# Two chained attention layers on one core: the squares of the next image's transpose sent a step sooner, and turned in place

## The chip, the cores and the metric

The kernel runs on one core of a Trainium2 chip. The metric is the device time of one execution in microseconds. All data are 32-bit floats.

## The reference

Eight images of 32 x 32 pixels with 256 channels pass through two attention layers. N = 1024 pixels of an image are the tokens.

```python
# layer 0, four heads, for each image
xf = x.reshape(B, N, C)
q, k, v = split(einsum('bnc,cd->bnd', xf, W_qkv).reshape(B, N, h, 3 * C), 3)
atten = softmax(einsum('bihd,bjhd->bijh', q, k) * C ** -0.5, axis=2)
res = einsum('bijh,bjhd->bihd', atten, v).reshape(B, N, h * C)
x = einsum('bnd,dc->bnc', res, W_out) + b_out + xf
# layer 1, one head with 32 channels for f and g
f, g, v = x @ Wf + bf, x @ Wg + bg, x @ Wh + bh
y = gamma * softmax(g @ f^T) @ v + x
```

## The kernel before

**Folded weights and seven products.** For each head of layer 0 the query and key weights are multiplied once into one 256 x 256 matrix (`wqk`), and the value and output weights into another (`wvo`). `fold_weights(h)` returns five tasks: turn q, turn k, turn v (L291: `pwq`, `pwk`, `pwv`), and two multiplications (L307: `pwqk`, `pwvo`). The larger products are made as 2 x 2 blocks with seven block products and sums of blocks in place of eight products. The helper `seven` (L222) holds this: its matmuls are all on line 235 and its additions on VectorE all on line 252, so they are told apart by tile names. In `psx`, `psy` and `psz` (scores), `psx_q` and so on (queries) and `psx_y` and so on (attention times values) the letter is the PSUM bank; `e`, `u` and `v` are the intermediate sums in SBUF, and the result goes to `p`, `q` or `y`. Sums of operands come from VectorE: `xs` (L385, from x^T), `qs` (L492), `s`, `s2`, `s3`, `ss` (L560, from the exponentials), and `xt` (L401, from the rows of x, by `value_sums`). The profile shows `s2` and `s3` as `s` too.

**Steps.** The list `steps` holds pairs of a unit and a block of 512 query tokens. A unit is a head of layer 0 of an image, or the layer-1 attention of the image before. That one stands behind head 1 of the next image (for the seventh image, behind head 3 of the eighth). Layer 1 of the last image comes after the loop. In one step the scores of that unit and block are made, with the products of the step before and the projections (`po`, L617) of the step before that.

**Order.** On TensorE, VectorE and ScalarE the order of instructions is the program's own. For each step the loop collects tasks with a place, a number on a scale where the six score tasks stand at 0, 2, 4, 6, 8 and 10, sorts them by place and calls them:

```python
        for _, _, t in sorted(places, key=lambda x: x[:2]):
            t()
```

A VectorE instruction that waits thus holds all VectorE work behind it. DMAs are all issued from SyncE (SP in the profile) in one queue; where they stand in it, and which buffer of a pool a tile gets, a scheduler decides. A DMA waits on SP for its source, for the release of the tile that its destination takes, and for one of eight completion semaphores to come free.

**x^T.** Layer 0 needs x and its transpose `x0T` (tag `xT`, two buffers, shared with `x1T`, the transpose of layer 0's output). Image 0's is made on TensorE (`transpose_rows`). For the others `turn_rows` moves squares of 32 x 32 elements by DMA to the place that they have in the transpose, and VectorE then turns each square with a 32 x 32 transpose. The squares land in a scratch tile, the still unused query tile of the next image's head 0 (`q`, two buffers). The moves (L358) are 16 DMAs per image; the four transposes (L364) read `q` and write `x0T`. All this belongs to step (head 3, block 0), and is followed there by the four `key_sums` (L385). The same function also turns layer 0's output for layer 1, with the tile `fg` as scratch.

**Row sums.** `Layer0.sums` reduces the sums of a block of exponentials over the partitions on GpSimd (L573), sends a row of it to memory (`line`, L577) and reads it back as columns (`st`, L580). `invert` (L586) takes the reciprocals, which `project` multiplies in (L628).

Of the kernel before, what the change touches and what calls it, by code (L numbers as in the profile page):

```python
# [16 lines left out]
P = 128  # L17
# [3 lines left out]
def kernel(  # L21
# [51 lines left out]
    nc = tc.nc  # L73
    B, H, W, C = x.shape
    N = H * W
    HEADS = w_qkv.shape[1] // (3 * C)
    CK = w_f.shape[1]
    CC = C // P
    NT = N // P
    NB = 512  # L80
# [28 lines left out]
    def tile_of(tag, shape, name):  # L109
        return pools[tag].tile(shape, F32, tag=tag, name=name)  # L110


    rows, rows1 = {}, {}

    def load_x(b, parts=1):
        t = tile_of("rows", [P, NT, C], f"x_{b}")
        n = HT // parts
        for k in range(NBLK):
            for i in range(parts):
                nc.sync.dma_start(  # L120
                    t[:, k * HT + i * n : k * HT + (i + 1) * n, :].rearrange("p t c -> p (t c)"),
                    x_v[b][:, k, ts(i, n * C)],
                )
        rows[b] = t
# [156 lines left out]
    def fold_weights(h):  # L281

        wT, hold = [], []
        folded[h] = []

        def turn(i, what):
            w, _ = weights[h]
            pt = tile_of("psm", [P, NB], f"pw{what}_{h}")
            for d in range(CC):
                for c in range(CC):  # L290
                    nc.tensor.transpose(  # L291
                        pt[:, d * C + c * P : d * C + (c + 1) * P],
                        w[:, c, i * C + d * P : i * C + (d + 1) * P],
                        ident,
                    )
            if i != 1:
                hold.append(tile_of("y", [P, N], f"w{what}T_{h}"))
            t = hold[-1][:, ts(i % 2, NB)]
            copy_on(i, t, pt)
            wT.append(t.rearrange("p (d c) -> p d c", d=CC))  # L300

        def multiply(i, what):
            wqT, wkT, wvT = wT
            pm = tile_of("psm", [P, NB], f"p{what}_{h}")
            for c in range(CC):
                for d in range(CC):
                    nc.tensor.matmul(  # L307
                        pm[:, ts(c, C)],
                        lhsT=(wqT, wvT)[i][:, d, ts(c, P)],
                        rhs=wkT[:, d, :] if i == 0 else weights[h][1][:, d, :],  # L310
                        start=(d == 0),
                        stop=(d == CC - 1),
                    )
            t = const.tile([P, CC, C], F32, tag=f"{what}{h}", name=f"{what}{h}")
            copy_on(i, t.rearrange("p c e -> p (c e)"), pm)
            folded[h].append(t)
            if i == 0:
                t4 = const.tile([P, 4, P], F32, tag=f"wt{h}", name=f"wt{h}")
                sums = [t4[:, k, :] for k in range(4)]
                blocks = [t[:, c, ts(e, P)] for c in range(CC) for e in range(CC)]  # L320
                run(sum_b(sums, *blocks))
                wblocks[h] = b_operands(blocks, sums)

        tasks = [partial(turn, i, what) for i, what in enumerate(("q", "k", "v"))]
        tasks += [partial(multiply, i, what) for i, what in enumerate(("wqk", "wvo"))]
        return tasks
# [16 lines left out]

        return [partial(task, k, c) for k in range(NBLK) for c in range(CC)]

    def turn_rows(b, src, dst, layer, scratch):

        Q = 32  # L350

        def move(a):
            to, rows_v = (
                t.rearrange("p u n -> p (u n)").rearrange("p (s q) -> p s q", q=P)
                for t in (scratch(), src[b])
            )
            for q in range(P // Q):
                nc.sync.dma_start(to[ts(q, Q), :, ts(a, Q)], rows_v[ts(a, Q), :, ts(q, Q)])  # L358

        def piece(k, c):  # L360
            if b not in dst:
                dst[b] = tile_of("xT", [P, CC, N], f"x{layer}T_{b}")
            squares = scratch()[:, k, :].rearrange("p (t c q) -> p t c q", c=CC, q=P)
            nc.vector.transpose(  # L364
                dst[b][:, c, ts(k, NB)].rearrange("p (t q) -> p t q", q=P), squares[:, :, c, :]
            )

        return (
            [partial(move, a) for a in range(P // Q)],
            [partial(piece, k, c) for k in range(NBLK) for c in range(CC)],  # L370
        )

# [409 lines left out]
    def run(*lists):  # L782
        for l in lists:
            for t in l:
                t()
# [42 lines left out]
    turn_q, turn_k, turn_v, *multiply = fold_weights(0)  # L828
    sums = key_sums(0)
    run(transpose_rows(0, rows, xT_of, 0), [turn_q, turn_k, sums[0], turn_v], sums[1:3])  # L830
    run(multiply, sums[3:], queries, qsums)

    def is_l0(s):
        return s is not None and isinstance(s[0], Layer0)
# [1 line left out]
    def step(k):  # L836
        return steps[k] if 0 <= k < len(steps) else None
# [4 lines left out]
    for i, (a, blk) in enumerate(steps):  # L842
        l0 = isinstance(a, Layer0)
        one, two, nxt = step(i - 1), step(i - 2), step(i + 1)
        places = []

        def put(tasks, *at):
            assert len(tasks) == len(at)
            places.extend(zip(at, range(len(places), len(places) + len(at)), tasks))

        if l0:
            put(a.scores(blk), 0, 2, 4, 6, 8, 10)
        else:
            tasks, pieces = a.scores(blk)
            put(tasks, *((0.5, 2.4) if blk == 0 else (0.5, 2)))
            put(pieces, *((1.6, 3.9, 6.2, 6.5, 7.4, 8.4, 8.6) if blk == 0 else
                          (0.9, 2.7, 4.2, 5, 6.2, 6.8, 7.5)))
        if is_l0(two):
            u, k = two
            put(u.products_of[k][2:], 1 if l0 else 0)  # L860
            put([partial(u.invert, k)], 2.9 if l0 or blk == 1 else 1.9)
            put(u.project(k), *((3, 7) if l0 else (2, 6) if blk == 0 else (3, 7)))
        if is_l0(one):
            u, k = one
            sums, keys = u.sums(k)
            u.products_of[k] = u.products(k)
            put(sums[:2] + sums[3:], *((2.2, 3.2, 4.2) if l0 else (0.8, 2.2, 4.5)))
            put(sums[2:3], 5.2 if l0 else 5.5)
            put(keys, *((6.2, 8.2) if l0 else (7.6, 9.6)))
            put(u.products_of[k][:2], *((5, 9) if l0 else (4, 7)))  # L870
        elif one is not None:
            put(one[0].products(one[1]), *((3, 5, 7, 9) if l0 else (1, 4, 6, 8)))
        if i == 0:
            fold = fold_weights(1) + fold_weights(2) + fold_weights(3)
            put(fold, -2, -1, *[0.9 + 0.6 * n for n in range(len(fold) - 2)])
        if i == 1:
            put([partial(nc.vector.tensor_scalar, bh_sb, bh_sb, gamma_sb, None, ALU.mult)], 8.5)

        if is_l0(nxt) and blk == NBLK - 1:
            queries, qsums = nxt[0].queries()  # L880
            put(queries, *((2.5, 4.5, 6.5) if not l0 else
                            (1.5, 2.5, 4.5) if is_l0(two) else (0.5, 2.5, 5.5)))
            put(qsums, *((6.7, 6.9, 7.3, 7.6) if not l0 else
                          (5.4, 6.4, 7.2, 7.4) if is_l0(two) else (6.4, 7.2, 7.3, 7.4)))

        if l0 and a.h == 0 and blk == 0:
            put(residual(a.b), 5.3, 6.3, 7.3, 7.4)
        if l0 and a.h == 0 and blk == 1:
            put(value_sums(a.b), 1.4, 2.4, 3.4, 4.4)
        if l0 and a.h == 2 and blk == 0 and a.b + 1 < B:  # L890
            load_x(a.b + 1)
        if l0 and a.h == HEADS - 1 and blk == 0 and a.b + 1 < B:
            moves, pieces = turn_rows(a.b + 1, rows, xT_of, 0, step(i + 2)[0].q_tile)
            put(moves, 0.1, 0.2, 0.3, 0.4)
            put(pieces, 3.4, 4.4, 5.4, 5.6)
            put(key_sums(a.b + 1), 6.4, 6.6, 7.2, 7.4)

        if l0 and a.b > 0 and a.h == behind(a.b) - 1:
            if blk == 0:
                moves, pieces = turn_rows(a.b - 1, rows1, x1T_of, 1, step(i + 2)[0].fg_tile)  # L900
                put(moves, 0.1, 0.2, 0.3, 0.4)
                put(pieces, 5.4, 6.4, 7.2, 7.4)
            else:
                put(nxt[0].queries(), 1.4, 1.5, 3.5)
        if not l0 and blk == 0:
            put(a.values(), 0.9, 1, 3, 5, 8)
        if nxt is None:
            put(transpose_rows(B - 1, rows1, x1T_of, 1), 8.1, 8.2, 8.3, 8.4)
            put(final.queries(), 9, 9.1, 9.3)
        for _, _, t in sorted(places, key=lambda x: x[:2]):  # L910
            t()
# [136 lines left out]
```

## Time and profile before

| what | value |
|---|---|
| time of three runs, median (lowest to highest) | 2374.21 us (2373.25 to 2375.3) |
| span of the profiled execution | 2373.4 us |
| VectorE busy | 1616.1 us (68%) |
| ScalarE busy | 589.8 us (25%) |
| GpSimd busy | 236.4 us (10%) |
| matmul instructions | 10384 |
| matmul 128 x 128 by 128 x 256 | 0.379 us |
| VectorE tensor_tensor, 128 x 512 | 0.68 to 0.69 us |
| VectorE tensor_tensor, 128 x 1024 | 1.22 us |
| VectorE transpose, 128 x 512 | 0.70 us (28 for `x0T`) |
| issue of one 64 KB move on SP | 0.63 us, 112 for `q`, 112 for `fg` |
| landing of such a move after its issue | 2.3 us (median) |

Busy time is the sum over an engine's instructions. "Idle before" an instruction is the time that its engine stood still just ahead of it, and the name behind the arrow is what ended that time. Where a row has one releaser, the instruction named there finished last. The end of a matmul is modelled, so a TensorE row's duration of several matmuls reaches beyond the start of the next group; the spacing of starts is what counts. The granted TensorE clock was full for the whole span.

### The profile page before, as it was taken

To read this page: it belongs to the slowest core of one execution; us is meant where nothing else is said; L and a number is where in the kernel's file an instruction comes from. 1 tells how busy PE (TensorE), PEld (TensorE's weight loads), DVE (VectorE), ACT (ScalarE), POOL (GpSimd) and SP (SyncE) were. 2 spreads that over 40 slices of the span, in tenths; PEclk is the share of its full clock that TensorE was granted. 3 is DMA by queue.
4 is the path that set the end of the run, shared out by engine and by line. 5 is a ranking of instruction groups with operands and counts; after the bars stand their busy time and mean duration, and the time that the engine had idled before them with its cause. 6 is when DMAs were issued, how large, how long until landed. Compare 5 with 4: busy or idle time off the path is not lost.

```text
span 2373.4 us, 25982 instructions
## 1 busy us (share of the span) xinstructions
PE 2342.1 (99%) x10384; PEld 1923.1 (81%) x10384; DVE 1616.1 (68%) x2533; ACT 589.8 (25%) x945; POOL 236.4 (10%) x93
## 2 busy tenths in 40 slices
PE   8999999999999999999999999999999999999999
PEld 6888888778878788787887878878788787888877
DVE  5667777577775667757777567675776757766665
ACT  2222223222232122322223222232122322222232
POOL 0111110011110111101111011110011101001110
PEclk9999999999999999999999999999999999999999
DMA  3001010010100101001010010100101001000100
GB/s 118 1 1 18 1 36 1 18 18 10 27 1 18 19 19 19 1 18 19 19 18 1 19 18 19 18 1 18 19 19 19 1 22 15 1 1 1 19 10 29
DMA packets 161809, 38.34 MB, mean 16 GB/s; under 512 B 154320, under 2 KB 156368, under 8 KB 161680
## 3 DMA queue, kind: packets, MB, share of 16 engines
q1 hardware_dynamic: 161680, 36.59, 7.5%
q8 instruction: 84, 1.38, 0.2%
q14 instruction: 45, 0.37, 0.0%
HBM read 13.37 MB, written 8.52 MB: 9 GB/s over the span
## 4 chain that ended last, share of the span: by engine, by line
PE 86%; DVE 8%; SPq 3%; issue 1%; DMA 1%; POOL 1%; ACT 0%; DVEq 0%; POOLq 0%; ACTq 0%
PE psy L235 12%; PE psy_y L235 12%; PE pa_l L767 9%; PE po L617 8%; PE psx L235 8%; PE psz L235 8%; PE psx_y L235 8%; PE psz_y L235 8%; PE psy_q L235 3%; SPq L358 3%; PE psx_q L235 2%; PE psz_q L235 2%; PE pr_v_l L446 2%; PE pm_fg L426 1%; PE ps_l L688 1%; DVE m L565 1%
## 5 line engine op out<-in xcount | busy, mean ns | idle before, releaser
L573 POOL PARTITION_ALL_REDUCE rb<-rs x64 | 206.9, 3233 | 1908.3 <-DVE rs L571 1908.3
L521 ACT ACTIVATE p<-p 128x1024 f32<-128x1024 f32 x128 | 135.3, 1057 | 573.3 <-DVE p L252 573.3
L235 PE MATMUL psy<-qs,xs 128*128 128x256 f32 x1024 | 264.2, 380 | 12.1 <-DVE u L252 6.2
L235 PE MATMUL psx<-q,x0T 128*128 128x256 f32 x1024 | 262.8, 379 | 0.0
L235 PE MATMUL psz<-q,xs 128*128 128x256 f32 x1024 | 262.8, 379 | 0.0
L235 PE MATMUL psy_y<-s,xt 128*128 128x256 f32 x1024 | 242.4, 380 | 1.4 <-DVE xt L401 1.2
L617 PE MATMUL po<-wvo,y 128*128 128x256 f32 x1024 | 242.0, 379 | 0.0
L235 PE MATMUL psx_y<-p,x 128*128 128x256 f32 x1024 | 241.9, 379 | 0.0
L767 PE MATMUL pa_l<-v_l,s_l 128*128 128x257 f32 x1024 | 231.7, 381 | 2.3 <-DVE y L252 1.9
L235 PEld LDWEIGHTS psx<-q,x0T 128*128 128x128 f32 x1024 | 194.4, 190 | 43.0 <-issue 18.7
L235 PEld LDWEIGHTS psy<-qs,xs 128*128 128x128 f32 x1024 | 193.4, 190 | 43.4 <-DVE u L252 9.0
L617 PEld LDWEIGHTS po<-wvo,y 128*128 128x128 f32 x1024 | 194.5, 190 | 40.0 <-issue 15.1
L767 PEld LDWEIGHTS pa_l<-v_l,s_l 128*128 128x128 f32 x1024 | 193.7, 190 | 39.0 <-issue 12.7
L235 PEld LDWEIGHTS psx_y<-p,x 128*128 128x128 f32 x1024 | 194.6, 190 | 34.1 <-issue 8.6
L235 PEld LDWEIGHTS psy_y<-s,xt 128*128 128x128 f32 x1024 | 192.1, 190 | 31.9 <-issue 4.0
L235 PEld LDWEIGHTS psz<-q,xs 128*128 128x128 f32 x1024 | 194.6, 190 | 26.4
L252 DVE TENSOR_TENSOR u<-psy,e 128x512 f32<-128x512 f32 x128 | 88.3, 690 | 143.7 <-ACT e L258 75.0
L264 ACT ACTIVATE p<-psx 128x512 f32<-128x512 f32 x128 | 76.4, 597 | 409.4 <-PE psx L235 409.3
L252 DVE TENSOR_TENSOR v<-psy,e 128x512 f32<-128x512 f32 x128 | 87.9, 687 | 104.4 <-PE psy L235 104.2
L235 PE MATMUL psy<-qs,x0T 128*128 128x256 f32 x512 | 132.1, 380 | 3.2 <-DVE v L252 3.2
L628 DVE SCALAR_TENSOR_TENSOR x<-po,inverse,x 128x256 f32<-128x256 f32 x256 | 112.0, 479 | 17.3 <-PE po L617 7.7
L235 PE MATMUL psz_y<-ss,x 128*128 128x256 f32 x512 | 120.9, 379 | 0.0
(110 smaller groups left out, 3048.0 us busy)
## 6 DMA issues: line engine op xcount, KB each, us to landing
out_dram<-x SPq DMA_DIRECT2D x15, 512.0 KB, 2.6
x<-in_x_dram SPq DMA_DIRECT2D x14, 512.0 KB, 4.6
q<-x SPq DMA_DIRECT2D x112, 64.0 KB, 2.3
fg<-x SPq DMA_DIRECT2D x112, 64.0 KB, 2.3
w<-in_L_conv_W_qkv_dram SPq DMA_DIRECT2D x4, 768.0 KB
x<-in_x_dram SPq DMA_DIRECT2D x4, 256.0 KB, 4.1
w<-in_L_conv_W_out_dram SPq DMA_DIRECT2D x4, 256.0 KB, 8.6
line<-rb SPq DMA_DIRECT2D x64, 2.0 KB
```

Of the source, the lines that this page charges most:

```text
L235: nc.tensor.matmul(banks[k][:, ts(i, w)], lhsT=lhsT, rhs=rhs, start=first and n == 0, stop=True, skip_group_check=True,)
L252: nc.vector.tensor_tensor(dst, shaped(banks[k]), shaped(other), ALU.add)
L264: copy(outs["11"](), shaped(banks["x"]))
L358: nc.sync.dma_start(to[ts(q, Q), :, ts(a, Q)], rows_v[ts(a, Q), :, ts(q, Q)])
L426: nc.tensor.matmul(pm[:m], lhsT=w()[:, c, d * P : d * P + m], rhs=src()[:, c, ts(k, NB)], start=(c == 0), stop=(c == CC - 1),)
L446: nc.tensor.matmul(pm[:, ts(j, C)], lhsT=src()[:, c, ts(2 * t2 + j, P)], rhs=w()[:, c, :], start=(c == 0), stop=(c == CC - 1),)
L521: exp(both, both)
L565: tt(m, t[:, :, 0:2, :], t[:, :, 2:4, :], ALU.add)
L573: nc.gpsimd.partition_all_reduce(t, r.rearrange("p e i -> p (e i)"), P, bass_isa.ReduceOp.add)
L617: nc.tensor.matmul(pm[:, ts(j, C)], lhsT=self.y[blk][:, c, ts(2 * t2 + j, P)], rhs=folded[self.h][1][:, c, :], start=(c == 0), stop=(c == ...
L628: nc.vector.scalar_tensor_tensor(acc, pm[:, ts(j, C)], inverse[:, n : n + 1], acc, ALU.mult, ALU.add)
L767: nc.tensor.matmul(pm[:, : C + 1], lhsT=p[:, j, ts(ti, P)], rhs=v[:, j, : C + 1], start=(j == 0), stop=(j == NT - 1),)
```

## The change

Three things change.

1. For the next image's `x0T` (not for layer 1's `x1T`), `turn_rows` is called without scratch. Its moves go into the `x0T` tile itself, split by channel half: 32 DMAs of 32 KB for 16 of 64 KB. They belong to step (head 2, block 1) and not to (head 3, block 0). The four transposes read and write the same 128 x 512 piece of `x0T`. In step (head 3, block 0) they stand at places 0.4, 1.4, 2.4 and 4.4 (before: 3.4, 4.4, 5.4, 5.6), and the first key sum at 5.4 (before: 6.4), the second at 6.4 (before: 6.6).
2. The four sums `xt` of image 0 are made two in step 0 and two in step 1; before, all four in step 1. Those of other images are not moved.
3. The first two tasks of head 1's folding come between the second and the third task of head 0's queries, ahead of the loop; the third stands at -1 in step 0, and the others follow at the same distances as before.

```diff
-    def turn_rows(b, src, dst, layer, scratch):
+    def turn_rows(b, src, dst, layer, scratch=None):
...
-        def move(a):
-            to, rows_v = (
-                t.rearrange("p u n -> p (u n)").rearrange("p (s q) -> p s q", q=P)
-                for t in (scratch(), src[b])
-            )
+        def end():
+            if b not in dst:
+                dst[b] = tile_of("xT", [P, CC, N], f"x{layer}T_{b}")
+            return dst[b]
+
+        def flat(t):
+            return t.rearrange("p u n -> p (u n)").rearrange("p (s q) -> p s q", q=P)
+
+        def move(a, c=None):
+            to, rows_v = flat(end() if scratch is None else scratch()), flat(src[b])
+            if c is not None:
+                to, rows_v = to[:, ts(c, NT), :], rows_v[:, c::CC, :]
             for q in range(P // Q):
                 nc.sync.dma_start(to[ts(q, Q), :, ts(a, Q)], rows_v[ts(a, Q), :, ts(q, Q)])
 
         def piece(k, c):
-            if b not in dst:
-                dst[b] = tile_of("xT", [P, CC, N], f"x{layer}T_{b}")
-            squares = scratch()[:, k, :].rearrange("p (t c q) -> p t c q", c=CC, q=P)
-            nc.vector.transpose(
-                dst[b][:, c, ts(k, NB)].rearrange("p (t q) -> p t q", q=P), squares[:, :, c, :]
-            )
+            to = end()[:, c, ts(k, NB)]
+            if scratch is None:
+                nc.vector.transpose(to, to)
+            else:
+                squares = scratch()[:, k, :].rearrange("p (t c q) -> p t c q", c=CC, q=P)
+                nc.vector.transpose(to.rearrange("p (t q) -> p t q", q=P), squares[:, :, c, :])
...
-    run(multiply, sums[3:], queries, qsums)
+    fold = fold_weights(1) + fold_weights(2) + fold_weights(3)
+    run(multiply, sums[3:], queries[:2], fold[:2], queries[2:], qsums)
+    first_sums = value_sums(0)
...
         if i == 0:
-            fold = fold_weights(1) + fold_weights(2) + fold_weights(3)
-            put(fold, -2, -1, *[0.9 + 0.6 * n for n in range(len(fold) - 2)])
+            put(fold[2:], -1, *[0.9 + 0.6 * n for n in range(len(fold) - 3)])
+            put(first_sums[:2], 8.4, 9.4)
         if i == 1:
+            put(first_sums[2:], 1.4, 3.4)
...
-        if l0 and a.h == 0 and blk == 1:
+        if l0 and a.h == 0 and blk == 1 and a.b > 0:
             put(value_sums(a.b), 1.4, 2.4, 3.4, 4.4)
...
+        if l0 and a.h == 2 and blk == 1 and a.b + 1 < B:
+            moves, squares = turn_rows(a.b + 1, rows, xT_of, 0)
+            put(moves, *range(1, 9))
         if l0 and a.h == HEADS - 1 and blk == 0 and a.b + 1 < B:
-            moves, pieces = turn_rows(a.b + 1, rows, xT_of, 0, step(i + 2)[0].q_tile)
-            put(moves, 0.1, 0.2, 0.3, 0.4)
-            put(pieces, 3.4, 4.4, 5.4, 5.6)
-            put(key_sums(a.b + 1), 6.4, 6.6, 7.2, 7.4)
+            put(squares, 0.4, 1.4, 2.4, 4.4)
+            put(key_sums(a.b + 1), 5.4, 6.4, 7.2, 7.4)
```

More of the change, by code (lines that the diff above doesn't have):

```diff
@@ L360, in piece @@
         def piece(k, c):
-            if b not in dst:
-                dst[b] = tile_of("xT", [P, CC, N], f"x{layer}T_{b}")
-            squares = scratch()[:, k, :].rearrange("p (t c q) -> p t c q", c=CC, q=P)
-            nc.vector.transpose(
-                dst[b][:, c, ts(k, NB)].rearrange("p (t q) -> p t q", q=P), squares[:, :, c, :]
-            )
+            to = end()[:, c, ts(k, NB)]
[4 more added lines that the diff above has]
+                nc.vector.transpose(to.rearrange("p (t q) -> p t q", q=P), squares[:, :, c, :])
         return (
-            [partial(move, a) for a in range(P // Q)],
+            [partial(move, a, c) for a in range(P // Q)
+             for c in ((None,) if scratch else range(CC))],
             [partial(piece, k, c) for k in range(NBLK) for c in range(CC)],
@@ L891 @@
             load_x(a.b + 1)
+        if l0 and a.h == 2 and blk == 1 and a.b + 1 < B:
+            moves, squares = turn_rows(a.b + 1, rows, xT_of, 0)
+            put(moves, *range(1, 9))
         if l0 and a.h == HEADS - 1 and blk == 0 and a.b + 1 < B:
-            moves, pieces = turn_rows(a.b + 1, rows, xT_of, 0, step(i + 2)[0].q_tile)
-            put(moves, 0.1, 0.2, 0.3, 0.4)
-            put(pieces, 3.4, 4.4, 5.4, 5.6)
-            put(key_sums(a.b + 1), 6.4, 6.6, 7.2, 7.4)
+            put(squares, 0.4, 1.4, 2.4, 4.4)
+            put(key_sums(a.b + 1), 5.4, 6.4, 7.2, 7.4)
         if l0 and a.b > 0 and a.h == behind(a.b) - 1:
             if blk == 0:
-                moves, pieces = turn_rows(a.b - 1, rows1, x1T_of, 1, step(i + 2)[0].fg_tile)
+                moves, turned = turn_rows(a.b - 1, rows1, x1T_of, 1, step(i + 2)[0].fg_tile)
                 put(moves, 0.1, 0.2, 0.3, 0.4)
-                put(pieces, 5.4, 6.4, 7.2, 7.4)
+                put(turned, 5.4, 6.4, 7.2, 7.4)
             else:
```

## The prediction

> **What bounds the kernel now.** I read the busy table first, then TensorE's waits, then the timeline around one of those waits.
>
> ```profile
> PE 2342.1 (99%) x10384; PEld 1923.1 (81%) x10384; DVE 1616.1 (68%) x2533; ACT 589.8 (25%) x945; POOL 236.4 (10%) x93
> ```
>
> TensorE is busy for 2342.1 of 2373.4 us. The change neither adds nor removes a matmul, so only the 31.3 us of idle can move. The view of who waited for whom says where most of it lies (total, times, longest):
>
> ```profile
> PE psy L235 <- DVE u L252: 6.2, 7, 1.0
> PE psy L235 <- DVE p L252: 4.6, 6, 1.8
> PE psy L235 <- DVE v L252: 3.2, 7, 0.5
> PE psy L235 <- DVE qs L492: 1.3, 1, 1.3
> PE psy_y L235 <- DVE xt L401: 1.2, 1, 1.2
> ...
> DVE x0T L364 <- DMA q<-x: 27.1, 7, 5.1
> ```
>
> There are eight images, so seven hand-overs to a next image, and the first three rows and the last come six or seven times each. Filtered to windows, they all fall in step (head 3, block 0), where the next image's x^T is turned. The timeline of the second hand-over shows the mechanism (start, duration, engine, line; in brackets the idle before):
>
> ```profile
> 498.01 9.35 SPq L358 DMA_DIRECT2D q<-x  x14
> ...
> 504.30 1.22 DVE L560 TENSOR_TENSOR s<-ss,p 128x1024 f32<-128x1024 f32 x1
> ...
> 505.63 1.60 PEld L235 LDWEIGHTS psy_y<-s,xt 128*128 128x128 f32 x8
> 505.74 1.89 PE L235 MATMUL psy_y<-s,xt 128*128 128x256 f32 x8
> ...
> 509.14 0.71 DVE L364 STREAM_TRANSPOSE x0T<-q 128x512 f32<-128x512 f32 x1 [3.63 <-DMA q<-x]
> ...
> 509.78 0.65 DVE L252 TENSOR_TENSOR p<-psy,e 128x512 f32<-128x512 f32 x1
> ...
> 510.49 1.13 PE L235 MATMUL psy<-qs,xs 128*128 128x256 f32 x4 [0.27 <-DVE p L252]
> ...
> 516.07 1.13 PE L235 MATMUL psy<-qs,xs 128*128 128x256 f32 x4 [0.99 <-DVE u L252]
> ...
> 521.11 1.13 PE L235 MATMUL psy<-qs,x0T 128*128 128x256 f32 x4 [0.46 <-DVE v L252]
> ```
>
> The sixteen square DMAs go out one after another up to 507.36 and the last lands at 509.02. VectorE reaches the first transpose at 505.5, stands 3.63 us, and everything behind it is late: the read of a PSUM bank (p), then u, then v. Each holds TensorE once.
>
> **What the Trainium skill says.** "Perfetto Trace Analysis", section "Tensor Engine Instruction (MATMUL, LD_WEIGHTS)", says ACT and DVE are strict FIFO; the trace agrees, since p had its inputs by 504.2 (its psz group ran at 503.15) and ran at 509.78 behind the transpose. The same page, "DMA Instruction — HWDGE (DVE, Sync)", says that the profiled DMA instruction ends when the sequencer is free and does not contain the data movement: here 0.63 us of issue beside 2.3 us to landing. "DMA: Bandwidth & Descriptors", section "Rules for kernel authors", advises issuing early and waiting late; that is this edit. "VectorE: DVE Perf Modes", section "The three transpose paths", limits a VectorE transpose to 32x32 blocks; the rows show 0.70 us for 128x512.
>
> **The change part by part.**
>
> *Squares sooner (images 1 to 7).* 16 moves of 64 KB into the q tile become 32 of 32 KB into the x^T tile, and nothing on VectorE waits for them any more. In the built program image 1's moves stand right behind the load of x_1 (issued at 20.18 us), over 100 us ahead of their transposes. For images 2 to 7 the first waits for the last pr_v matmul of the layer-1 unit, which reads the old contents of that x^T slot: for image 2 the group at 408.49, done by 410.4. At the 0.67 us spacing of the larger moves 32 take 21.4 us, and they are done near 436, 60 us before the transposes. Removed per hand-over: 2.4 to 5.1 us of VectorE standing. On TensorE that is 6.2 + 4.6 + 3.2 = 14.0 us. A restart costs more than the idle shows: the four matmuls at 516.07 take 0.97 to the next group, where others take 0.86, so 20 restarts x 0.11 = 2.2. Together **16.2 us**, the most that this part can return.
>
> *Transposes earlier.* In VectorE's order the four transposes move from behind s, ss and s to: after u; after the second y; ahead of the reciprocal; behind the second ss. Walking the second hand-over with the row's durations (independent instructions start 0.09 us before the former ends): T0 at 496.4 and T1 at 499.4 fall in idle of 0.85 and 1.3 us. T2 does not: ss starts at 502.10, T2 at 503.23, so the reciprocal, the two x and s move by 0.62, and s ends at 506.14 instead of 505.52. The weights of psy_y<-s were loaded at 505.63, that is, as soon as s was there, so this is a **new wait**: TensorE starts at about 506.20 instead of 505.74, 0.46 and a restart of 0.11 to 0.2, say 0.6. The first hand-over has the same spacing (s at 214.28, psy_y at 215.72). 7 x 0.6 = **4.3 us lost**. Going on: p at 506.1 and 506.6, ss 507.2, T3 508.4, u_y 509.5 (behind ACT's exp), s 509.8, xs 511.0; u waits for its own matmuls and runs at 511.8 (TensorE needs it at 515.0), v at 516.4 (needed at 519.3). So none of p, u and v holds TensorE: net 16.2 - 4.3 = **11.9 us**.
>
> *In-place form.* No row shows it. Nearest is the same instruction from q, 0.70 us; bounds are the 0.61 spacing of dense tensor_tensor rows and twice the row, 1.4. I take 0.70; twice makes the new wait 1.3 us, 5 us more in all.
>
> *SP's queue.* 16 more issues x 7 x 0.67 = at most 75 us (a half-size issue costs between st's 0.36 and 0.63); SP waits 1483.8 us for the row sums alone. But order matters. In Layer1's block 0 seven moves stand ahead of the line DMA of head 1, block 1, and three between line and st:
>
> ```profile
> 418.12 0.23 SPq L577 DMA_DIRECT2D line<-rb  x1
> 419.31 0.36 SPq L580 DMA_DIRECT2D st<-line  x1
> 426.34 0.17 DVE L586 RECIPROCAL inverse<-st 128x4 f32<-128x4 f32 x1
> ```
>
> The seven end at 410.4 + 4.7 = 415.1, before the sums at 418.1: nothing lost. Three cost 2.0, so st goes out at 420.4 and lands (2.1 us) at 422.5, 3.8 ahead of its reader. The 22 left end at 435.5, before the output DMA's condition at 441.43. Cost: nothing, hidden by that slack. POOL's order is unchanged.
>
> *Image 0.* Two of the four xt sums move to idle VectorE time in step 0 (1.12 us idle ahead of 51.40), so the 1.2 us wait of psy_y for xt goes, with its restart **1.3 gained**. The folding of head 1 starts two tasks earlier: pwq and pwk fill the 0.78 us in which psy_q waited for v_q, but q and qs depend on v_q, not on these, so psy still starts at 26.18 and the idle there grows from 1.29 to 1.9. Pwv has moved ahead of it (0.43 us gained), but further on pwq, pwk and pwv now follow directly on a score group, and pwv waits for the copy of pwq behind v and p on VectorE, about 1.3 us where before 0.35 stood. Net **0.6 lost**, bounds 1.5 gained and 2.5 lost.
>
> Sum: -11.9 - 1.3 + 0.6 = **-12.6 us**; on the profiled span 2373.4 that is 2360.8, and on the median of the runs, 2374.2, it is **2361.6 us**.
>
> **The rivals.**
> 1. *New wait twice as large, or dear in-place transposes.* For: s is needed as soon as it is made. Gain 12.6 - 5 = 7.6: 2366.6 us.
> 2. *Hidden anyway.* The stretch holds the same VectorE work, and if u and v are late by its density rather than by the 3.63 us, only the p waits go (4.6 + 0.7), about eaten by the new 4.3: with image 0 the time is 2373 us. Against: the walk leaves VectorE 2 to 3 us ahead at u and v.
> 3. *Slower: st lands late.* Image 2 to 7's moves share SP and the DMA engines with st. If moves drained one at a time (2.3 us each), the ten ahead of it would hold st's data until 410.4 + 23 + 2.1 = 435.5, and L586 would stand 9.2 us with x, r_l and s_l behind it and TensorE waiting for PSUM. It decides from a delay of 4 us on, and turns the sum above 6 us. About 8 us on TensorE x 6 - 12.6 = +35: 2410 us. Against: 14 moves sent 0.67 apart landed 2.29 us after the last issue, so they overlap.
> 4. *The moves stay late.* If the x^T slot were freed later than the built order says, the transposes would wait as before: 2373 us.
>
> **How the numbers follow.** Forecast 0.72, rival 1 0.14, rivals 2 and 4 together 0.08, rival 3 0.06. The forecast's own spread is image 0's bounds (about -2 to +2) and the new wait (3 to 5 us, or nothing if s slips in): 2357 to 2365. With rival 1 and an edge for unknown sizes the range is 2356 to 2369 us. A difference of 0.2% (4.7 us) is about what can be told from none here: faster 0.87, same 0.07, slower 0.06.
>
> **What would show it.** The row "x0T <- DMA" goes from VectorE's waits; p, u and v go from TensorE's; a row psy_y <- s appears with 7 entries of about 0.5 us; psy_y <- xt is gone; L586 waits for no DMA; TensorE busy stays 2342. I am wrong if u and v keep holding TensorE, if L586 waits, or if the idle that went from the hand-overs turns up in image 0's first 50 us.

## The result, and the profile after

The changed kernel takes 2358.94 us (median of six runs, 2357.61 to 2360.93) beside 2374.9 us for the kernel before on the same chips (six runs, 2373.25 to 2376.75). The ratio is 0.9933, with a 95% interval of 0.992 to 0.9946. That is 16.0 us less; 12.6 us had been predicted. The profiled span fell by 16.5 us, from 2373.4 to 2356.9.

The busy line of the changed kernel's page:

```profile
PE 2336.5 (99%) x10384; PEld 1923.2 (82%) x10384; DVE 1617.1 (69%) x2533; ACT 590.7 (25%) x945; POOL 236.6 (10%) x93
```

VectorE does the same work as before, to 1 us. TensorE's busy time is 5.6 us lower with the same 10384 matmuls, which the prediction had excluded; the reason is further down. TensorE's waits in the changed kernel (total, times, longest; the row of the load of x at the start, and rows of 0.4 us and less, are left out):

```profile
...
PE psy_y L235 <- DVE s L569: 2.4, 7, 0.3
PE pa_l L776 <- DVE y L252: 1.9, 7, 0.3
PE psy L235 <- DVE qs L501: 1.7, 1, 1.7
PE psy L235 <- DVE v L252: 0.8, 1, 0.8
PE pwk L291 <- ACT wvo L172: 0.8, 1, 0.8
PE pwv L291 <- ACT wqT L172: 0.7, 1, 0.7
...
```

The rows for p and u are gone, and so are the seven waits for v. The one wait for v in this list is another, at 50.08 us in image 0, and new. No row "x0T <- DMA" stands in VectorE's waits any more. The new row is psy_y's wait for s, seven times. The timeline of the second hand-over shows the same places as before:

```profile
494.35 0.70 DVE L371 STREAM_TRANSPOSE x0T<-x0T 128x512 f32<-128x512 f32 x1
...
497.35 0.70 DVE L371 STREAM_TRANSPOSE x0T<-x0T 128x512 f32<-128x512 f32 x1
...
501.20 0.70 DVE L371 STREAM_TRANSPOSE x0T<-x0T 128x512 f32<-128x512 f32 x1
...
502.86 1.22 DVE L569 TENSOR_TENSOR s<-ss,p 128x1024 f32<-128x1024 f32 x1
...
504.22 1.96 PE L235 MATMUL psy_y<-s,xt 128*128 128x256 f32 x8 [0.34 <-DVE s L569]
...
508.61 1.03 PE L235 MATMUL psy<-qs,xs 128*128 128x256 f32 x4
...
512.92 1.03 PE L235 MATMUL psy<-qs,xs 128*128 128x256 f32 x4
...
517.24 1.03 PE L235 MATMUL psy<-qs,x0T 128*128 128x256 f32 x4
```

The first two transposes fill idle VectorE time, the third stands ahead of s, and the three psy groups that had waited 0.27, 0.99 and 0.46 us start without a wait. SP's queue ahead of this hand-over, and the reader of st:

```profile
408.39 4.51 SPq L366 DMA_DIRECT2D x0T<-x  x7
416.10 0.24 SPq L586 DMA_DIRECT2D line<-rb  x1
416.38 1.90 SPq L366 DMA_DIRECT2D x0T<-x  x3
418.39 0.54 SPq L589 DMA_DIRECT2D st<-line  x1
418.97 15.19 SPq L366 DMA_DIRECT2D x0T<-x  x22
...
424.32 0.17 DVE L595 RECIPROCAL inverse<-st 128x4 f32<-128x4 f32 x1
```

This is the queue that the prediction laid out, 2 us earlier: seven moves ahead of the line DMA, three ahead of st, the rest done by 434, and the reciprocal 5.9 us after st's issue with no wait.

**Where the time came from.** I compared the start of the same matmul group in both profiles; "lead" is how much earlier the changed kernel is.

| place | lead after it | gained there |
|---|---|---|
| first query product of image 0, ahead of any changed instruction | 1.67 | 1.67 |
| last scores of image 0's first step | 0.15 | -1.52 |
| first psy_y (waited for xt before) | 1.35 | 1.20 |
| hand-overs 1 to 7 | 2.03, 3.97, 6.51, 8.46, 10.57, 13.26, 16.71 | 0.68, 1.94, 2.54, 1.95, 2.11, 2.69, 3.45 |

The hand-overs give 15.4 us. Image 0 gives -0.3, and the first 1.67 us are not the change's: in the eleven profiles, of kernels whose TensorE work does not differ up to that group, it starts between 14.26 and 16.98 us.

### The profile page after: what moved, and what is told of

Read it like the earlier page. It is cut to its first block, busy times and chain, and to the rows that moved or that the text cites. A ratio compares the mean times of both kernels' runs of the same rounds, so it can differ in the third digit from the quotient of the medians.

```text
span 2356.9 us, 26075 instructions
## 1 busy us (share of the span) xinstructions
PE 2336.5 (99%) x10384; PEld 1923.2 (82%) x10384; DVE 1617.1 (69%) x2533; ACT 590.7 (25%) x945; POOL 236.6 (10%) x93
## 4 chain that ended last, share of the span: by engine, by line
PE 95%; DVE 4%; DMA 0%; ACT 0%; issue 0%; SPq 0%; DVEq 0%; ACTq 0%
PE psy L235 14%; PE psy_y L235 14%; PE pa_l L776 9%; PE psx L235 9%; PE psz L235 9%; PE po L626 9%; PE psx_y L235 9%; PE psz_y L235 9%; PE psy_q L235 4%; PE psx_q L235 2%; PE psz_q L235 2%; PE pr_v_l L455 2%; PE pm_fg L435 1%; PE ps_l L697 1%; DVE s_l L758 1%; DVE s L569 0%
## 5 line engine op out<-in xcount | busy, mean ns | idle before, releaser
L776 PEld LDWEIGHTS pa_l<-v_l,s_l 128*128 128x128 f32 x1024 | 193.7, 190 | 39.0 <-issue 12.6
L258 ACT COPY e<-psx 128x512 f32<-128x512 f32 x128 | 73.9, 577 | 202.3 <-PE psx L235 202.3
```

Source lines behind the costliest of these rows:

```text
L258: nc.scalar.copy(scratch("e"), banks["x"])
L776: nc.tensor.matmul(pm[:, : C + 1], lhsT=p[:, j, ts(ti, P)], rhs=v[:, j, : C + 1], start=(j == 0), stop=(j == NT - 1),)
```

## The experiments

**Which part carries the gain.** The squares part alone, as a diff against the changed kernel (the condition that moves image 0's four sums back to step 1 is left out):

```diff
-    run(multiply, sums[3:], queries[:2], fold[:2], queries[2:], qsums)
-    first_sums = value_sums(0)
+    run(multiply, sums[3:], queries, qsums)
...
-            put(fold[2:], -1, *[0.9 + 0.6 * n for n in range(len(fold) - 3)])
-            put(first_sums[:2], 8.4, 9.4)
+            put(fold, -2, -1, *[0.9 + 0.6 * n for n in range(len(fold) - 2)])
...
-            put(first_sums[2:], 1.4, 3.4)
...
```

> The squares part alone: moves into the x^T tile and transposes in place at the new places, with image 0's row sums and folding in their old order. Theory: the seven hand-overs carry the whole gain, 15.4 us by the two profiles (0.68 + 1.94 + 2.54 + 1.95 + 2.11 + 2.69 + 3.45), so about 2359.5 us, ratio 0.9935, with the same seven waits of psy_y for s. Rival: image 0's part carries some 4 us of the 16, then about 2363 us.

Measured: 2358.83 us, ratio 0.9937 (0.9923 to 0.995). The squares part is the whole gain: counted from the first query product, so that the start is left out, its profile gains 15.3 us on the kernel before, and that of the changed kernel 15.0. Its profile has the same row of seven waits for s.

The second run puts only the folding order of the changed kernel into the kernel before.

> The kernel before with only the first two folding tasks of head 1 ahead of the third query task. Theory: this part loses about 1.5 us between the first query product and the end of image 0's first step (1.67 us of lead shrinks to 0.15 us there in the two profiles), so about 2376.4 us, ratio 1.0006, and the wait of psy for qs is 1.7 us. Rival: it is what made the first 16 us of the profile after 1.67 us shorter, then 2373 us. The difference is near what five rounds can tell; the profile's first 52 us decide.

Measured: 2376.18 us, ratio 1.0006 (0.9998 to 1.0015), so the timed runs show no difference. The profile does: between the first query product and the last scores of the first step the kernel loses 1.52 us against the kernel before, the same amount as in the changed kernel. Its TensorE waits, those rows that differ from the kernel before in image 0:

```profile
...
PE psy L235 <- DVE v L252: 4.0, 8, 0.8
...
PE psy L235 <- DVE qs L492: 1.7, 1, 1.7
...
PE pwk L291 <- ACT wvo L172: 0.8, 1, 0.8
PE pwv L291 <- ACT wqT L172: 0.7, 1, 0.7
...
```

The eighth wait for v and that of pwv are new; pwk's is longer than the one of the kernel before (0.2 us) and at another place, and psy's for qs is 0.4 us longer. The start of this profile was slow, not fast (first query product at 16.98 us): the rival falls. Over all profiles the six with this order start the product between 14.26 and 16.98 us, the five without it between 14.37 and 16.28.

**Is it density or the DMA?** Transposes back at the old places, squares still early:

```diff
-            put(squares, 0.4, 1.4, 2.4, 4.4)
-            put(key_sums(a.b + 1), 5.4, 6.4, 7.2, 7.4)
+            put(squares, 3.4, 4.4, 5.4, 5.6)
+            put(key_sums(a.b + 1), 6.4, 6.6, 7.2, 7.4)
```

> The changed kernel with the transposes and key sums back at their places of before (3.4, 4.4, 5.4, 5.6), so that none stands ahead of the sum s that psy_y needs; the squares still come early. Theory: the standing of VectorE for the DMA was the whole cause, so p, u and v hold TensorE no more, and the wait of psy_y for s goes too: 7 x 0.58 = 4.1 us less than the changed kernel, about 2355 us. Rival: the stretch is too dense at the old places, and u and v still wait (9.4 us of idle and 14 restarts of 0.28): about 2368 us.

Measured: 2355.09 us, ratio 0.9917 (0.9904 to 0.9931). The same stretch of the second hand-over:

```profile
503.95 1.22 DVE L569 TENSOR_TENSOR s<-ss,p 128x1024 f32<-128x1024 f32 x1
505.08 0.70 DVE L371 STREAM_TRANSPOSE x0T<-x0T 128x512 f32<-128x512 f32 x1
505.40 1.89 PE L235 MATMUL psy_y<-s,xt 128*128 128x256 f32 x8
...
514.03 1.03 PE L235 MATMUL psy<-qs,xs 128*128 128x256 f32 x4
...
518.35 1.03 PE L235 MATMUL psy<-qs,x0T 128*128 128x256 f32 x4
```

No group waits: the first transpose follows s directly, where in the kernel before it stood 3.63 us for the DMA. The standing was the whole cause; the same VectorE work at the same places fits. Over the seven hand-overs this profile's lead over the kernel before grows by 19.4 us, against 15.4 in the changed kernel. Moving the transposes earlier brought nothing and cost the wait for s.

**The price of the new wait.** Only the third transpose goes behind s:

```diff
-            put(squares, 0.4, 1.4, 2.4, 4.4)
+            put(squares, 0.4, 1.4, 3.3, 4.4)
```

> The changed kernel with its third transpose at place 3.3 instead of 2.4, that is, behind the sum s. Theory: the seven waits of psy_y for s go, each worth its idle of 0.34 us and another 0.24 us that no idle column shows: 4.1 us, about 2355 us, while the lead of each hand-over grows by 0.58 us. Rival: a wait costs only its idle, 2.4 us: about 2356.5 us. Second rival: p, which now comes 0.62 us later, holds TensorE instead: 2359 us.

Measured: 2355.61 us, ratio 0.9924 (0.991 to 0.9937). The row psy_y <- s is gone and no row comes in its place. Against the changed kernel the lead grows by 0.57 or 0.58 us at each of the seven hand-overs, one after the other. That settles the price per wait, which the timed difference of 3.3 us, between both expectations, could not. The second rival falls, since no row for p appears.

**What brings the squares early: the place or the destination?** First the moves at the old place, still into the x^T tile:

```diff
-        if l0 and a.h == 2 and blk == 1 and a.b + 1 < B:
-            moves, squares = turn_rows(a.b + 1, rows, xT_of, 0)
-            put(moves, *range(1, 9))
         if l0 and a.h == HEADS - 1 and blk == 0 and a.b + 1 < B:
+            moves, squares = turn_rows(a.b + 1, rows, xT_of, 0)
+            put(moves, *[0.1 + 0.01 * n for n in range(8)])
```

> The changed kernel with the moves put back into step (head 3, block 0), still into the x^T tile. Theory: what brings the squares early is the destination, whose buffer is free early, and not the place in the step list, so that SP's order, the moves at 27 us and from 408 us, and the time stay those of the changed kernel, about 2359 us. Rival: the place decides; then VectorE stands for the DMA again and the time is near the kernel before with the new wait on top, about 2375 us.

Measured: 2359.27 us, ratio 0.9932 (0.9917 to 0.9947), that is, the time of the changed kernel. Its SP timeline:

```profile
27.45 21.48 SPq L366 DMA_DIRECT2D x0T<-x  x32
...
410.37 4.51 SPq L366 DMA_DIRECT2D x0T<-x  x7
418.08 0.24 SPq L586 DMA_DIRECT2D line<-rb  x1
```

These are the places of the changed kernel (27.26 and 408.39 us there), up to the later start of this profile. In SP's own waits one row says what holds the moves of images 2 to 7:

```profile
SPq L366 <- PE pr_v_l L455: 135.8, 6, 22.6
```

It is the release of the x^T tile by the layer-1 unit that read its old contents. Then the other half: the moves a step sooner, into the q tile of before.

```diff
+        if l0 and a.h == 2 and blk == 1 and a.b + 1 < B:
+            moves, squares = turn_rows(a.b + 1, rows, xT_of, 0, step(i + 3)[0].q_tile)
+            put(moves, 9.1, 9.2, 9.3, 9.4)
         if l0 and a.h == HEADS - 1 and blk == 0 and a.b + 1 < B:
-            moves, pieces = turn_rows(a.b + 1, rows, xT_of, 0, step(i + 2)[0].q_tile)
-            put(moves, 0.1, 0.2, 0.3, 0.4)
-            put(pieces, 3.4, 4.4, 5.4, 5.6)
+            put(squares, 3.4, 4.4, 5.4, 5.6)
```

> The kernel before with its moves put a step sooner, into step (head 2, block 1), but still into the q tile. Theory: that buffer is free only when head 2's last scores have read it, so the moves go out where they did, VectorE stands 2.4 to 5.1 us in each hand-over, and the time stays 2375 us. Rival: the sooner place alone brings them early; then 19 us less, about 2356 us.

Measured: 2373.94 us, ratio 0.9996 (0.9987 to 1.0004): no difference from before. VectorE's row and SP's queue are those of before:

```profile
DVE x0T L364 <- DMA q<-x: 26.9, 7, 4.6
```

```profile
494.10 0.24 SPq L577 DMA_DIRECT2D line<-rb  x1
494.44 1.27 SPq L358 DMA_DIRECT2D q<-x  x2
495.80 0.57 SPq L580 DMA_DIRECT2D st<-line  x1
496.43 9.35 SPq L358 DMA_DIRECT2D q<-x  x14
```

The two together show it: the place in the step list moves these DMAs not at all, and the destination does, by some 85 us in the second hand-over. Into the x^T tile a move goes out when that tile is released; the row above shows it. For the q tile the same reason fits but is not shown: there the moves stand in SP's queue behind the line DMA, and no wait of L358 itself is longer than 0.5 us. The new destination came with moves of half the size; that size alone was not run.

**How near is SP's queue?** Each move cut into four of 8 KB, 128 per image:

```diff
-                nc.sync.dma_start(to[ts(q, Q), :, ts(a, Q)], rows_v[ts(a, Q), :, ts(q, Q)])
+                parts = 4 if c is not None else 1
+                m = to.shape[1] // parts
+                for e in range(parts):
+                    nc.sync.dma_start(
+                        to[ts(q, Q), ts(e, m), ts(a, Q)], rows_v[ts(a, Q), ts(e, m), ts(q, Q)]
+                    )
```

> The changed kernel with each of its 32 moves per image cut into four of 8 KB (128 per image, 79 us of SP's time at 0.62 us each). Theory: SP's queue is nowhere near the path; the last moves go out near 490 us in the second hand-over, just ahead of the first transpose at 494, the st of head 1, block 1 is late by 0.6 us more than in the changed kernel against 3.5 us of slack, and the time is that of the changed kernel, 2359 us, or up to 2 us more if the last square lands late. Rival: SP is the next bound; the row sums behind the moves come late, L586's counterpart waits for st, and the time rises by 10 us or more.

Measured: 2359.36 us, ratio 0.9934 (0.9919 to 0.9949), the time of the changed kernel. The last moves before the second hand-over:

```profile
458.78 29.73 SPq L369 DMA_DIRECT2D x0T<-x  x45
488.62 0.52 SPq L728 DMA_DIRECT2D out_dram<-x  x1
489.19 8.93 SPq L369 DMA_DIRECT2D x0T<-x  x14
```

They run up to 498.1, later than expected, largely since an issue takes 0.66 us in its spacing at this size too. Still no VectorE row for x0T appears; the reciprocal of st waited once, 0.5 us, and no TensorE row came of it. Four times the issues cost nothing, so the changed kernel's 32 are far from the path.

**Image 0's sums alone** (`first_sums` at 8.4 and 9.4 in step 0 and at 1.4 and 3.4 in step 1, in the kernel before):

> The kernel before with image 0's four xt sums made two in step 0 and two in step 1, nothing else. Theory: the one wait of psy_y for xt goes, 1.2 to 1.5 us between 51 and 67 us of the profile, and nothing in step 0 is held by the two sums there: about 2373.7 us, a difference that the timed runs hardly tell; the profile decides. Rival: the two sums in step 0 delay the p that follows them and a TensorE wait appears there, so that nothing is gained: 2375 us.

Measured: 2373.04 us, ratio 0.9994 (0.9985 to 1.0003); the runs can't tell it from no change. In the profile the row psy_y <- xt is gone, the lead over the kernel before jumps by 1.20 us at the first psy_y (from -0.28 to 0.92), and nowhere else in the first 240 us.

**The version that follows.** The third transpose behind s, the folding in its old order, the sums in two steps (the diffs above):

> The changed kernel with its third transpose behind the sum s, and head 1's folding in its order of before; image 0's row sums stay in two steps. Theory: the 4.1 us of the seven waits of psy_y for s and the 1.5 us that the folding order lost between the first query product and the end of image 0's first step add up: about 2353.5 us. Rival: without the folding order the first step's sums collide and only the 4.1 us come: about 2355 us. The profile's lead over the changed kernel at the end of the first step tells them apart.

Measured: 2354.89 us, ratio 0.9913 (0.99 to 0.9927), the fastest median, and faster than the changed kernel. Its slowest run, 2355.51 us, lies below the fastest of the changed kernel, 2357.61. Its lead over the changed kernel grows by 1.52 us from the first query product to the end of the first step, as expected. The timed runs do not separate it from the kernel with the old places (2355.09) or the one with the third transpose later (2355.61). The profiles do, counted from the first query product: it gains 20.6 us on the kernel before, those two 19.05 each.

## Why the prediction was right, and where it was off

*The cause.* Right. VectorE stood for the squares, and TensorE paid for it through p, u and v. With the squares early and everything else at its place (old places) all three are gone, so density was no part of it, and rival 2 falls. Rival 4 falls with the SP timeline. The walk came true as well: with the 2.03 us of lead added, u ran at 511.77 and v at 516.29 us, where it had 511.8 and 516.4. One reading was off without harm: the p at 509.78 reads the psy group at 502.29, and not the psz group at 503.15, which feeds the p behind it.

*"The most that this part can return", 16.2 us.* This is the term that was mis-sized; it is 19.4 us. The prediction took the idle column, 14.0 us, and 0.11 us for each of 20 restarts. The second hand-over of the kernel before shows what was left out: psx starts at 514.05, and the next group normally follows 0.86 us later, at 514.91, but psy started at 516.07. That is 1.16 us late where the column says 0.99. The column counts from the modelled end of the matmuls, 1.03 us after the start, so it misses 0.17 us per wait; with the 0.11 a wait costs 0.28 us more than its idle. 14.0 + 20 x 0.28 = 19.6, and 15.4 gained + 7 x 0.58 lost = 19.4. The old places, where neither these waits nor the new one stand, measure the term directly: 19.4, that is 0.27 us beyond the idle per wait. Hand-over by hand-over it fits too: the seventh had 3.22 us of idle, 3.22 + 3 x 0.28 - 0.58 = 3.48, measured 3.45. The same 0.27 us counts as busy, which explains most of the fall in TensorE's busy time: 20 x 0.27 less 7 x 0.24 for the new waits is the 3.7 us by which it fell from the end of image 0's first step on. Another 2.0 us of busy time are missing ahead of the first query product, where nothing was changed.

*The new wait, 0.6 us each, 4.3 us.* Right: its price is 0.57 or 0.58 us, 4.0 in all, shown by taking it away (7 x 0.6 is 4.2; the 4.3 is a slip of 0.1). Here the prediction had counted from start to start, 0.46 us late and a restart, and not taken the idle, which is 0.34.

*The in-place transpose at 0.70 us.* Right: 0.702 us on average beside 0.696 from the q tile. Rival 1 falls.

*SP's queue and rival 3.* Right that st stays ahead of its reader. Even 128 moves per image change no time.

*Image 0's sums, 1.3 us.* Measured 1.20, alone and together.

*The folding, 0.6 us lost.* It lost 1.52, within the bounds given. The steps up to the wait for qs came as worked out (1.73 us idle for 1.9). Behind it the walk had the wrong copy: pwv did not wait some 1.3 us for VectorE's copy of pwq but 0.72 us for ACT's of pwk, so that this place lost about 0.4 us, no more than pwv's own move had gained. The loss came from what the walk did not reach, the pwk at 40.43 that waits 0.76 us for ACT's copy, and the psy at 50.08 that waits 0.78 us for v. That the total stayed within the bounds is in part luck.

*What the change is called.* The prediction took the early moves from the built order without asking what made them early. It is the destination; "a step sooner" does nothing.

The sum: 15.4 for 11.9 at the hand-overs, -0.3 for +0.7 in image 0, together 15.0 for 12.6. Two misses of opposite sign stand in it: 3.5 us too little at the hand-overs, 1.0 too much in image 0. The rest of the 16.5 us between the spans lies in the first 16 us, ahead of the change; the interval of the runs' difference of 16.0 us holds the 15.0.

## What to carry to other kernels

When a DMA ends a wait of an in-order engine, look at what released the DMA: where a scheduler orders the queue, as here, the buffer that the transfer writes can set its time, and moving the call in the program then does nothing. Writing straight into the final tile can free the transfer by many steps. When such work comes early, leave the instructions that used to wait where they were, unless a walk shows that nothing behind them is needed as soon as it is made. And price a short TensorE wait by the spacing of group starts, not by the idle column.

## What the runs showed of the hardware

- The issue of a move costs SP about the same at any of these sizes: 0.63 us at 64 KB, 0.61 at 32 KB, 0.60 at 8 KB (medians), while the landing falls from 2.3 to 2.0 and 1.8 us.
- A TensorE wait of 0.26 to 1.77 us between groups of four matmuls cost 0.27 us beyond what the idle column shows (19.4 us for 20 waits with 14.0 of idle); a wait ahead of eight 128x256 matmuls cost 0.24 us beyond it (0.58 for 0.34).
- The first matmuls are slow for a time that differs between executions of the same instructions. The group of four pwq transposes took 1.08 us at 9.04 us in the profile before and 0.63 us at 8.90 us in the one after, and the first query product started between 14.26 and 16.98 us in eleven profiles. The cause was not tested.
